# Depthwise conv with 8 rows by 4 column phases of outputs and two column shifts

## The chip, the cores and the metric

The kernel runs on one core of a Trainium2 chip. Its time is the device time of one execution in microseconds (us); the profile is of one execution taken by the hardware profiler. Five engines work in order, each on its own queue: PE (matrix products), DVE, ACT, POOL (elementwise work) and SP (which issues most transfers). Sixteen DMA engines move data between the chip's memory (DRAM) and the on-chip memory.

## The reference, cut to what matters

Input x has 4 images of 128 channels, 128 x 128 pixels. Layer 0 runs attention in overlapping windows of 16 x 16 (step 14, so 9 bands of 9 windows per image), adds x, averages the overlaps (`merged`), and then:

```python
y = _ln(xf, ln2_g, ln2_b)
y = y @ w_p0 + b_p0                       # 128 -> 256 channels
ym = conv_general_dilated(ym, dw_k, window_strides=(1, 1), padding=[(2, 2), (2, 2)],
                          feature_group_count=HIDDEN)      # depthwise, 5 x 5
ym = batchnorm(ym)                        # over images and pixels
y = gelu(gelu(ym)) @ w_p2 + b_p2 + xf     # 256 -> 128 channels
```

Layer 1 has two 3 x 3 convolutions with quantised inputs and weights, each followed by a batch norm; the second adds its input (`identity`).

## The kernel before, in words

Everything is in float32 but layer 1's products, which are in fp8. There are four stages.

*Attention and conv.* A loop runs over 36 bands t, and within it over 9 windows j. The order of work on PE, ACT, DVE and SP is written by hand (`beside`, L881): in each window the scores of j, the values of j-1, and pieces of side work: the first layer norm of the next band (`ln1_chunks`, L478), the output projection, second layer norm and expansion to 256 channels of the band before (`post_chunks`, L531), and tiles of the depthwise conv (`conv_steps`, L615) of an image whose bands are all done. Images 0 and 1 are convolved beside nine bands each, image 2 beside five, and image 3 in three units: rows 0 to 63, 64 to 95 and 96 to 127, the last after the loop (`conv_rest`, L679).

The depthwise conv is done on PE as a banded product. Per channel, the 32 outputs of a column pair are 16 rows by 2 column phases (even, odd); the inputs that they need are 20 rows by 2 phases, `KD` = 40 rows of the contraction. A column shift of -1, 0 and +1 pairs covers the five columns, so there are three products per channel, accumulated in PSUM (`depthwise`, L592), over 8 groups of 16 rows and 64 column pairs, 512 columns. Two channels lie in the two halves of the partitions and four in the four column strips of the array, so eight products run beside each other; a tile (`conv_steps`, at 8 groups) holds 8 channels and 24 matmuls.

The expansion `p0` (L561) takes half a chunk (4 or 3 rows) and half of the channels; ACT adds the bias, splits even and odd columns and writes a tile y (L567; two buffers for each half of the channels, so four), which is stored to y_d in DRAM as rows of 64 values: 256 B pieces. The residual `xf` is stored to xf_d in whole chunks of rows. A conv tile loads its input from y_d (`input_of`, L607; four transfers per tile), ACT copies the result out of PSUM (L648), DVE takes its statistics (L652), and it is stored to cv_d, one 256 B piece for each output row and column phase.

Most transfers are issued by SP, in order. `flush` (L429) issues the stores that a piece of side work left, right after that piece.

*Gelu stage* (`gelu_stage`, L1182 on). 64 units of 8 image rows: load 1 MB of conv result and 0.5 MB of xf, two gelus on ACT, the product back to 128 channels on PE (L1228), bias and residual on DVE (L1236, which also interleaves even and odd columns), quantisation, and layer 1's first conv of the unit two steps earlier (`conv3x3`, L1155; its matmuls are L1164).

*Last stages* (`last_stages`, L1280 on). The second conv once over all units for the statistics, the conv of the unit three steps earlier each time, and then again for images 0 to 2 for the output, adding the identity and storing 0.5 MB per unit.

Of the kernel before, what the change touches and what calls it, by code (L numbers as in the profile page):

```python
# [14 lines left out]
P = 128  # L15
# [16 lines left out]
GR = 16  # L32
CW = P // 2
KD = 2 * (GR + 4)
NCK = 8

# [10 lines left out]
def layers(  # L47
# [42 lines left out]
    y2_d = [dram.tile([P + 4, 2, 2 * P, CW], F32, name=f"y2_d{b}") for b in range(B)]  # L90
    cv_d = [dram.tile([P // GR, 2 * P, GR * P], F32, name=f"cv_d{b}") for b in range(B)]

    dw_d = dram.tile([2 * NCK, KD, 3, 16 * 32], F32, name="dw_d")
    pad_d = dram.tile([2 * GR + 3, 7, 2 * P], F32, name="pad_d")
    band_d = dram.tile([32, 3, KD, 2 * P], F32, name="band_d")
# [74 lines left out]
    units = [(b, 0, P // GR) for b in range(B - 1)] + [(B - 1, g, n) for g, n in ((0, 4), (4, 2), (6, 2))]  # L170
# [14 lines left out]
    with ExitStack() as actx:  # L185
# [18 lines left out]
        y2t = [[y2p.tile([P, RB, 2, CW], F32, name=f"y2_{h}{n}") for n in range(2)] for h in range(2)]  # L204
# [4 lines left out]
        def scratch(n):  # L209

            return up.tile([P, 32 * CW], F32, name="u")[:, :n]

        def band_matrices():
# [6 lines left out]
            def zeros():  # L220
                zero = scratch(2 * 2 * 2 * CW)
                nc.gpsimd.memset(zero, 0.0)
                held["taps"] = taps = scratch(2 * P)[:N_TAPS]
                nc.sync.dma_start(out=taps, in_=dw_k.rearrange("c o i j -> (o i j) c"))
                n = (2 * GR + 3) * 7 * 2 * P // P
                nc.sync.dma_start(
                    out=pad_d.rearrange("y x c -> (y x c)").rearrange("(p n) -> p n", p=P),
                    in_=zero[:, :n],
                )
                held["zero"] = zero  # L230

            def edges(b):
                for d in (y2_d[b][0:2], y2_d[b][P + 2 :]):
                    nc.sync.dma_start(
                        out=d.rearrange("r e c x -> (r e c x)").rearrange("(p n) -> p n", p=P),
                        in_=held["zero"],
                    )

            def padded_taps():
                for dy in range(5):  # L240
                    nc.sync.dma_start(
                        out=pad_d[GR - 1 + dy, 1:6, :], in_=held["taps"][5 * dy : 5 * dy + 5, :]
                    )

            def by_outputs(ro):
                for eo in range(2):

                    nc.sync.dma_start(
                        out=band_d[2 * ro + eo].rearrange("s (r e) c -> s r (e c)", e=2),
                        in_=bass.AP(  # L250
                            pad_d.tensor,
                            pad_d[GR - 1 - ro, 1 - eo, 0:1].offset,
                            [[4 * P, 3], [7 * 2 * P, GR + 4], [1, 4 * P]],
# [32 lines left out]
            pieces = [(c, s) for c in range(0, 2 * P, 64) for s in range(3)]  # L286
            steps = [zeros, *each(edges, [(b,) for b in range(B)]), padded_taps, lambda: None]
            steps += each(by_outputs, [(ro,) for ro in range(GR)])
# [242 lines left out]
        def post_chunks(t, sel=None):  # L531
# [4 lines left out]
            for at, (r, n) in enumerate(finished(t)):  # L536
# [5 lines left out]
                def project(hh, r=r, n=n, at=at, held=held):  # L542
# [9 lines left out]
                    if hh:  # L552
                        store(
                            xf_d[b][:, (i * STEP + r) * P : (i * STEP + r + n) * P],
                            held["xf"][:, : n * P],
                        )
# [4 lines left out]
                def p0(h, hh, r=r, n=n // 2, held=held):  # L561
# [4 lines left out]
                    y2t[h].append(y)  # L566
                    nc.scalar.activation(  # L567
                        y[:, :n],
                        pm[:, : n * P].rearrange("p (r c e) -> p r e c", r=n, e=2),
                        AF.Identity, bias=bp0[:, h : h + 1],  # L570
                    )
                    store(
                        y2_d[b][row + 2 : row + n + 2, :, h * P : (h + 1) * P, :].rearrange(
                            "r e p x -> p (r e) x"
                        ),
                        y[:, :n].rearrange("p r e x -> p (r e) x"),
                    )

# [13 lines left out]
        def depthwise(outs, wt, ut, n):  # L592

            for j in range(n // 4):

                for s, (a, z) in ((1, (0, CW)), (0, (1, CW)), (2, (0, CW - 1))):
                    for half in range(2):
                        hs = slice(64 * half, 64 * half + KD)
                        for q in range(4):
                            c = 4 * j + q  # L600
                            nc.tensor.matmul(  # L601
                                outs[half][32 * q : 32 * q + 32, j, :, a:z],
                                wt[hs, s, c, :], ut[hs, :, c, a + s - 1 : z + s - 1],
                                start=(s == 1), stop=(s == 2),
                            )

        def input_of(b, g, ng, ch, n, a, z):  # L607

            return bass.AP(
                y2_d[b].tensor,  # L610
                y2_d[b][GR * g + a, 0, ch, 0:1].offset,
                [[2 * P * CW, 2 * (z - a)], [GR * 2 * 2 * P * CW, ng], [1, n * CW]],
            )

        def conv_steps(n, ahead=2):  # L615
# [3 lines left out]
            nc_ = min(8, 32 // ng)  # L619
# [4 lines left out]
            def load(at):  # L624
                k, jj, c = tiles[at]
                if c == 0:
                    W[k, jj] = up.tile([P, 3, 8, 32], F32, name="w")
                    weights(W[k, jj], k, jj, 1, nc.sync.dma_start)
                ut = up.tile([P, 32 * CW], F32, name="u")[:, : ng * nc_ * CW]
                U[at] = ut = ut.rearrange("p (g c x) -> p g c x", g=ng, c=nc_)  # L630
                for half in range(2):
                    ch = 32 * k + 16 * half + 8 * jj + c
                    for a, z in ((0, GR), (GR, GR + 4)):
                        nc.sync.dma_start(
                            out=ut[64 * half + 2 * a : 64 * half + 2 * z].rearrange(
                                "p g c x -> p g (c x)"
                            ),
                            in_=input_of(b, g0, ng, ch, nc_, a, z),
                        )

            def products(at):
# [4 lines left out]
                for half in range(2):  # L646
# [4 lines left out]
                    for j in range(nj):  # L651
# [3 lines left out]
                        ch = 32 * k + 16 * half + 8 * jj + c0 + 4 * j  # L655
                        store(
                            bass.AP(
                                cv_d[b].tensor,
                                cv_d[b][g0, ch, 0:1].offset,
                                [[CW, P], [2 * P * GR * P, ng], [1, CW]],  # L660
                            ),
                            cv[:, j],
# [16 lines left out]
        def conv_rest(n, w_t, u_t, c_t):  # L679
# [5 lines left out]
            at = GR + 2  # L685

            def load(k, a, z, g, m):
                for half in range(2):
                    ch = 32 * k + 16 * half
                    nc.sync.dma_start(  # L690
                        out=U[k][64 * half + 2 * a : 64 * half + 2 * z, g : g + m].rearrange(
                            "p g c x -> p g (c x)"
                        ),
                        in_=input_of(b, g0 + g, m, ch, 16, a, z),
                    )

            U = [u_t.tile([P, ng, 16, CW], F32, name=f"u{k}") for k in range(NCK)]
            W = [w_t.tile([P, 3, 16, 32], F32, name=f"w{k}") for k in range(NCK)]
            for k in range(NCK):
                weights(W[k], k, 0, 2, nc.gpsimd.dma_start)  # L700
            for k in range(early):
                load(k, 0, at, 0, 1)

            def late(k):
                if k < early:
                    load(k, 0, at, 1, 1)
                    load(k, at, GR + 4, 0, ng)
                else:
                    load(k, 0, GR, 0, ng)
                    load(k, GR, GR + 4, 0, ng)  # L710

            def step(k):
# [6 lines left out]
                for half in range(2):  # L719
# [9 lines left out]
                    for g in range(ng):  # L729
                        engine.dma_start(  # L730
                            out=bass.AP(
                                cv_d[b].tensor,
                                cv_d[b][g0 + g, 32 * k + 16 * half, 0:1].offset,
# [673 lines left out]
```

## Time and profile before

| | us |
|---|---|
| median of 3 runs | 3246.4 (3238.51 to 3248.32) |
| the profiled execution | 3249.98 |
| its span, first to last instruction | 3248.2 |

| group | count | busy us | mean ns |
|---|---|---|---|
| L1164 PE, layer 1's convs | 3168 | 700.3 | 381 |
| L784 PE, scores | 5184 | 413.6 | 417 |
| L567 ACT, y out of PSUM | 288 | 183.1 | 641 |
| L648 ACT, conv result out of PSUM | 256 | 132.4 | 563 |
| L867 DVE, reciprocal | 324 | 568.8 | 1756 |

A row of a group names the line, the engine, the operation, its output and inputs with their shapes, and how often it ran; then the union of its time, the mean of one, and the idle time of the engine before it with what ended it. PE lists a float32 matmul as two. A row of the timeline has the start, the length, the engine, the operation and, in brackets, how long the engine had been idle and what released it. The DMA share is the mean busy share of the 16 DMA engines. The clock is PE's granted clock, 1.00 being full.

ACT waited for stores of y to land (y_d<-y) 76 times, 111.9 us in all, at most 14.6. Most of the attention stage, from 525 us on, has conv tiles beside it; the gelu stage runs from about 2320 to 2795 us, the second conv's two passes from there to the end.

### The profile page before, as it was taken

How to read it: one execution, taken by the hardware profiler on the slowest of the kernel's cores; microseconds unless marked ns; L12 is line 12 of the kernel's file. 1: busy time of each engine (PE TensorE's matmuls, PEld its weight loads, DVE VectorE, ACT ScalarE, POOL GpSimd, SP SyncE). 2: the span in 40 equal slices, each digit the busy share in tenths (PEclk: the TensorE clock that was granted, in tenths of full speed). 3: DMA queues.
4: the chain of work that ended last, by engine and by line, in shares of the span. 5: the costliest groups of instructions: out<-in, count | busy, mean ns of one | idle time of the engine just before them, and what ended most of it. 6: DMA issues, size and time to landing. Idle time of an engine off the chain costs nothing.

```text
span 3248.2 us, 92154 instructions
## 1 busy us (share of the span) xinstructions
PE 3059.6 (94%) x39162; PEld 1480.1 (46%) x39162; DVE 2014.5 (62%) x3244; ACT 1988.5 (61%) x2658; POOL 840.9 (26%) x1058
## 2 busy tenths in 40 slices
PE   7999999999999999999888998876899999999998
PEld 4555544444444444444344444453544444444443
DVE  5777886766766777676555664542455555666543
ACT  5777777777776777677555655432477777433443
POOL 3444443333333333333222232211111111000000
PEclk9999999999999999999999998876799999999999
DMA  3555677888886888886898988857899999452398
GB/s 82 151 167 162 176 186 191 203 199 204 215 193 169 191 206 211 196 213 172 179 202 201 209 188 203 196 158 187 264 354 359 358 359 304 162 167 80 110 357 311
DMA packets 809891, 681.70 MB, mean 210 GB/s; under 512 B 580918, under 2 KB 695935, under 8 KB 809471
## 3 DMA queue, kind: packets, MB, share of 16 engines
q1 hardware_dynamic: 798879, 669.17, 75.8%
q8 instruction: 311, 5.10, 0.7%
q0 software_dynamic: 1024, 3.93, 0.5%
q10 hardware_dynamic: 9568, 2.61, 0.3%
q14 instruction: 109, 0.89, 0.1%
HBM read 408.72 MB, written 270.79 MB: 209 GB/s over the span
## 4 chain that ended last, share of the span: by engine, by line
PE 76%; DMA 9%; ACT 5%; issue 4%; SPq 3%; DVE 2%; ACTq 0%; POOL 0%; DVEq 0%; POOLq 0%
PE pc L1164 21%; PE pm L438 16%; PE sc L784 9%; PE pm L601 9%; PE po L847 8%; PE pb L1228 6%; PE po L855 3%; DMA y_d<-y 3%; PE pm L377 3%; ACT pt L792 2%; DMA u<-y_d 2%; DMA xn<-row 1%; SPq L451 1%; SPq L431 1%; ACT v L775 1%
## 5 line engine op out<-in xcount | busy, mean ns | idle before, releaser
L867 DVE RECIPROCAL rd<-po 128x256 f32<-128x256 f32 x324 | 568.8, 1756 | 439.1 <-PE po L855 438.5
L1164 PE MATMUL pc<-q,wq 128*128 128x512 fp8e4 x3168 | 700.3, 381 | 5.1 <-DVE q L1176 5.1
L792 ACT ACTIVATE pt<-sc 128x1024 f32<-128x1024 f32 x648 | 628.2, 1025 | 119.1 <-PE sc L784 63.2
L802 POOL TENSOR_TENSOR sm<-pt 128x512 f32<-128x512 f32 x324 | 415.7, 1283 | 1047.3 <-ACT pt L792 727.0
L1164 PEld LDWEIGHTS <-wq 128*128 128x128 fp8e4 x3168 | 309.0, 98 | 406.7 <-issue 38.9
L784 PE MATMUL sc<-q,kr 32*128 32x256 f32 x5184 | 413.6, 417 | 27.3 <-ACT pt L792 27.1
L601 PE MATMUL pm<-u,w 40*32 40x504 f32 (+5 forms) x7680 | 369.6, 503 | 41.7 <-DMA u<-y_d 29.7
L784 PEld LDWEIGHTS sc<-q,kr 32*128 32x128 f32 x5184 | 254.1, 191 | 286.4 <-issue 177.1
L847 PE MATMUL po<-pt,v 128*32 128x256 f32 x5184 | 364.9, 401 | 10.0 <-DVE part L871 6.9
L648 ACT COPY c<-pm 128x512 f32<-128x512 f32 (+1 forms) x256 | 132.4, 563 | 272.3 <-PE pm L601 243.3
L438 PE MATMUL pm<-xn,wp 128*32 128x512 f32 (+1 forms) x2304 | 248.1, 553 | 44.6 <-ACT y L567 42.6
L567 ACT ACTIVATE y<-pm,vectors 128x512 f32<-128x512 f32 (+1 forms) x288 | 183.1, 641 | 166.0 <-DMA y_d<-y 111.9
L802 DVE TENSOR_TENSOR sm<-pt 128x512 f32<-128x512 f32 x324 | 244.2, 754 | 35.8 <-ACT pt L792 35.8
L438 PE MATMUL pm<-xn,wqkv 128*32 128x512 f32 (+1 forms) x2304 | 245.3, 548 | 4.9 <-ACT v L775 3.5
L601 PEld LDWEIGHTS pm<-u,w 40*32 40x32 f32 x7680 | 147.6, 112 | 223.1 <-issue 153.0
L652 DVE BATCH_NORM_STATS2 st<-c 128x6 f32<-128x512 f32 (+2 forms) x320 | 160.9, 550 | 134.8 <-ACT c L648 134.3
L1228 PE MATMUL pb<-cv,wp 128*128 128x512 f32 x512 | 232.1, 596 | 4.9 <-ACT cv L1219 4.9
L847 PEld LDWEIGHTS po<-pt,v 128*32 128x32 f32 x5184 | 140.5, 112 | 186.5 <-issue 103.5
L1172 DVE BATCH_NORM_STATS2 st<-pc 128x6 f32<-128x512 f32 x256 | 165.7, 689 | 84.7 <-PE pc L1164 84.7
L855 PE MATMUL po<-sm,ones 128*32 128x256 f32 x2592 | 206.1, 389 | 0.0
L874 POOL TENSOR_TENSOR ob<-ob,part 128x32 f32<-128x32 f32 x288 | 127.2, 442 | 230.6 <-DVE part L871 224.8
L438 PE MATMUL pm<-wqkv,yr 128*32 128x128 f32 x5184 | 176.3, 273 | 1.2 <-issue 1.2
(157 smaller groups left out, 3394.2 us busy)
## 6 DMA issues: line engine op xcount, KB each, us to landing
cv<-cv_d SPq DMA_DIRECT2D x64, 1024.0 KB
u<-y_d SPq DMA_DIRECT2D x234, 256.0 KB
cv_d<-c SPq DMA_DIRECT2D x192, 256.0 KB
y_d<-y SPq DMA_DIRECT2D x160, 256.0 KB
xn<-row SPq DMA_DIRECT2D x76, 512.0 KB
xfl<-xf_d SPq DMA_DIRECT2D x64, 512.0 KB
id_d<-y SPq DMA_DIRECT2D x64, 512.0 KB
idt<-id_d SPq DMA_DIRECT2D x64, 512.0 KB
```

Source lines behind the costliest of these rows:

```text
L438: nc.tensor.matmul(out[m], w[:, m], v, start=True, stop=True)
L567: nc.scalar.activation(y[:, :n], pm[:, : n * P].rearrange("p (r c e) -> p r e c", r=n, e=2), AF.Identity, bias=bp0[:, h : h + 1],)
L601: nc.tensor.matmul(outs[half][32 * q : 32 * q + 32, j, :, a:z], wt[hs, s, c, :], ut[hs, :, c, a + s - 1 : z + s - 1], start=(s == 1), stop ...
L784: nc.tensor.matmul(sc[h // 2][:, h % 2, kc, :].rearrange("p (r c) -> p r c", c=RS), region(kr, j)[hs, kc * P : (kc + 1) * P], queries(j, h ...
L792: nc.scalar.activation(pt, sc[p], AF.Exp)
L802: add(sm, pt[:, :, 0, :], pt[:, :, 1, :], ALU.add)
L847: nc.tensor.matmul(po[hs, 0, :], v[:, kc, hs], pt[h // 2][:, h % 2, kc, :], start=(kc == 0), stop=(kc == 1),)
L855: nc.tensor.matmul(po[hs, 1, :], ones, sm[h // 2][:, h % 2, :], start=True, stop=True)
L867: nc.vector.reciprocal(rd, po[:, 1, :])
L1164: nc.tensor.matmul(pc[:, h], w[:, t, :], q1[b][:, r + dy : r + dy + RB, dx : dx + P], start=(t == 0), stop=(t == 8),)
L1172: nc.vector.bn_stats(st[:, 2 * n + h, :], pc[:, h])
L1228: nc.tensor.matmul(pb[:, m], wp2[:, h, :], cv[:, h, px], start=(h == 0), stop=(h == 1))
```

## The change

The conv's outputs are 8 rows by 4 column phases (`GR` 16 to 8, `NC` 4), its inputs 12 rows by 4 phases (`KD` 40 to 48), and two column shifts cover the five columns: two products for three. A channel of an image has 16 groups of 8 rows and 32 column quads, again 512 columns.

y_d has the order phase and row in the group, channel, group, 33 columns; a tile y has four phases of 33 columns in each row, with one zero column for the border, and each piece that is stored is 33 values, 132 B. Two of the four phases are written by ACT, two by DVE. A store that crosses a group of 8 rows is cut in two. A tile of the conv's input is, for whole images, one contiguous run of 4 channels x 17 groups x 33 columns on each partition (`fetch_input`). The conv's result goes to cv_d with 8 groups of one output row and phase side by side (1 KB pieces for whole images and rows 0 to 95 in part, 512 B for the last rows). xf_d has its rows in the same order, so it is stored in rows of 512 B.

In the later stages a unit of 8 rows is then the rows with the same place in their group (rows 0, 8, 16 ... of half an image). q1's rows are laid out so that the conv's neighbours are again contiguous blocks (`first_row`), the units run in the order 7, 0, 1, ... 6 in each half, the conv follows four units later (`LAG`) instead of two or three, and the output is stored in rows of 512 B.

```diff
-GR = 16
-CW = P // 2
-KD = 2 * (GR + 4)
+GR = 8
+NG = P // GR
+NC = 4
+CW = P // NC
+CX = CW + 1
+KD = NC * (GR + 4)
 NCK = 8
+LAG = 4
...
-    y2_d = [dram.tile([P + 4, 2, 2 * P, CW], F32, name=f"y2_d{b}") for b in range(B)]
-    cv_d = [dram.tile([P // GR, 2 * P, GR * P], F32, name=f"cv_d{b}") for b in range(B)]
+    y2_d = [dram.tile([NC * GR, 2 * P, NG + 1, CX], F32, name=f"y2_d{b}") for b in range(B)]
+    cv_d = [dram.tile([2, 2 * P, 32, NG // 2, CW], F32, name=f"cv_d{b}") for b in range(B)]
...
+                        row = i * STEP + r
+                        cut = min(n, GR - row % GR)
+                        for a, z in ((0, cut), (cut, n)):
+                            if z > a:
+                                g, ro = divmod(row + a, GR)
+                                store(
+                                    xf_d[b].rearrange("p (h o g c) -> p h o g c", h=2, o=GR, c=P)[
+                                        :, g // 8, ro : ro + z - a, g % 8, :
+                                    ],
+                                    held["xf"][:, a * P : z * P].rearrange("p (r c) -> p r c", c=P),
+                                )
...
+                    to = y[:, :n].rearrange("p r (a f x) -> p r a f x", a=2, x=CX)
+                    by = pm[:, : n * P].rearrange("p (r x a f) -> p r a f x", r=n, a=2, f=2)
                     nc.scalar.activation(
-                        y[:, :n],
-                        pm[:, : n * P].rearrange("p (r c e) -> p r e c", r=n, e=2),
-                        AF.Identity, bias=bp0[:, h : h + 1],
+                        to[:, :, 0, :, :CW], by[:, :, 0], AF.Identity, bias=bp0[:, h : h + 1]
                     )
-                    store(
-                        y2_d[b][row + 2 : row + n + 2, :, h * P : (h + 1) * P, :].rearrange(
-                            "r e p x -> p (r e) x"
-                        ),
-                        y[:, :n].rearrange("p r e x -> p (r e) x"),
+                    nc.vector.tensor_scalar(
+                        to[:, :, 1, :, 1:], by[:, :, 1], bp0[:, h : h + 1], None, ALU.add
                     )
+                    cut = min(n, GR - (row + 2) % GR)
+                    for a, z in ((0, cut), (cut, n)):
+                        if z > a:
+                            g, r0 = divmod(row + 2 + a, GR)
+                            store(
+                                y2_d[b][NC * r0 : NC * (r0 + z - a), h * P : (h + 1) * P, g, :].rearrange(
+                                    "q p x -> p q x"
+                                ),
+                                y[:, a:z].rearrange("p r (q x) -> p (r q) x", x=CX),
+                            )
...
-                for s, (a, z) in ((1, (0, CW)), (0, (1, CW)), (2, (0, CW - 1))):
+                for s in range(2):
                     for half in range(2):
                         hs = slice(64 * half, 64 * half + KD)
                         for q in range(4):
                             c = 4 * j + q
                             nc.tensor.matmul(
-                                outs[half][32 * q : 32 * q + 32, j, :, a:z],
-                                wt[hs, s, c, :], ut[hs, :, c, a + s - 1 : z + s - 1],
-                                start=(s == 1), stop=(s == 2),
+                                outs[half][32 * q : 32 * q + 32, j],
+                                wt[hs, s, c, :], ut[hs, c, : outs[half].shape[2], s : s + CW],
+                                start=(s == 0), stop=(s == 1),
                             )
...
+        def fetch_input(ut, b, g, ch, below):
+            n, ng = ut.shape[1:3]
+            rows = 4 if below else GR
+            for half in range(2):
+                to = ut[64 * half + NC * GR * below : 64 * half + NC * (GR * below + rows)]
+                src = y2_d[b][0 : NC * rows, ch + 16 * half : ch + 16 * half + n]
+                if ng > NG:
+                    m = (n * ng - below) * CX
+                    nc.sync.dma_start(
+                        out=to.rearrange("p c g x -> p (c g x)")[:, :m],
+                        in_=bass.AP(src.tensor, src.offset + below * CX, [src.ap[0], [1, m]]),
+                    )
...
-                                [[CW, P], [2 * P * GR * P, ng], [1, CW]],
+                                [[8 * CW, P], [2 * P * 32 * 8 * CW, gh], [1, ng // gh * CW]],
...
+    def first_row(k):
+        return {-1: 0, GR - 1: 1, 0: NG + 1, GR: NG + 2}.get(k, NG + 2 + NG * k)
...
-                if n >= 2:
-                    pc = conv3x3(ps_c, n - 2, wq[0])
+                if n >= LAG:
+                    pc = conv3x3(ps_c, n - LAG, wq[0])
...
-                if n >= 3:
-                    b, k = units[n - 3]
-                    pc = conv3x3(ps_d, n - 3, wq[1])
+                if n >= LAG:
+                    b, k = conv_units[n - LAG]
+                    pc = conv3x3(ps_d, n - LAG, wq[1])
...
-                    out=out[b, :, 2 * RB * k : 2 * RB * (k + 1), :].rearrange("c r w -> c (r w)"), in_=z
+                    out=out[b, :, k // GR * 64 + k % GR : k // GR * 64 + 64 : GR, :],
+                    in_=z.rearrange("p (r w) -> p r w", w=P),
```

Beside these, the preparation in the first ten bands follows the layout: 64 copies that build the bands of taps for 32, eight pieces of weights for twelve, zeros written to the borders of y_d in 132 B pieces, and the four y tiles cleared once at the start.

## The prediction

> **What bounds the kernel now.** I read the page first (shares, transfers, groups), then the busy time by stretches, then the timeline at the end of one band and at one long stall, and last the transfer records grouped by size.
>
> ```profile
> span 3248.2 us, 92154 instructions
> ...
> PE 3059.6 (94%) x39162; PEld 1480.1 (46%) x39162; DVE 2014.5 (62%) x3244; ACT 1988.5 (61%) x2658; POOL 840.9 (26%) x1058
> ...
> DMA packets 809891, 681.70 MB, mean 210 GB/s; under 512 B 580918, under 2 KB 695935, under 8 KB 809471
> ...
> L601 PE MATMUL pm<-u,w 40*32 40x504 f32 (+5 forms) x7680 | 369.6, 503 | 41.7 <-DMA u<-y_d 29.7
> ```
>
> PE is the bound, and the depthwise conv (L601) holds 369.6 us of it, with 75.6 us more in a group of its own at the end of attention. But most transfers are under 512 B: 539,648 of 256 B, half the stores of y, half those of the conv's result.
>
> ```profile
> 525.00:1015.00 490.00, 481.26 (x7786) 227.66 (x7776) 347.88 (x542) 353.21 (x536) 180.17 (x228) 1.00 0.84 198
> ...
> 1640.00:1930.00 290.00, 267.17 (x4120) 122.95 (x4118) 172.91 (x266) 175.44 (x269) 83.34 (x107) 0.95 0.89 204
> ...
> 2200.00:2330.00 130.00, 86.12 (x1961) 58.20 (x1958) 43.87 (x181) 37.75 (x54) 17.97 (x38) 0.63 0.75 200
> ...
> 3045.00:3248.00 203.00, 193.38 (x892) 86.46 (x889) 82.30 (x81) 78.91 (x67) 0.55 (x1) 0.99 0.86 311
> ```
>
> The columns are length, then PE, PEld, DVE, ACT, POOL busy, the clock, the DMA share and GB/s. While image 0 is convolved (from 525) PE is idle 9 us in 490, at a DMA share of 0.84 (0.87 in its full bands). Where image 2 goes through in five bands (from 1640), the share is 0.89 and PE loses 23 us and 5% of its clock. So the conv stretch lies close to a second limit, the transfers.
>
> ```profile
> 903.77 1.76 DVE L867 RECIPROCAL rd<-po 128x256 f32<-128x256 f32 x1 [0.66 <-PE po L855]
> ...
> 903.93 3.62 PE L438 MATMUL pm<-xn,wp 128*32 128x512 f32 x32
> ...
> 906.57 1.08 DVE L421 TENSOR_TENSOR xn<-xn,xf 128x384 f32<-128x384 f32 x2
> ...
> 908.73 9.95 SPq L431 DMA_DIRECT2D y_d<-y  x8
> ...
> 916.84 0.58 ACT L567 ACTIVATE y<-pm,vectors 128x384 f32<-128x384 f32 x1 [1.46 <-DMA y_d<-y]
> ...
> 917.71 0.58 ACT L567 ACTIVATE y<-pm,vectors 128x384 f32<-128x384 f32 x1 [0.29 <-DMA y_d<-y]
> ...
> 919.75 1.94 ACT L792 ACTIVATE pt<-sc 128x1024 f32<-128x1024 f32 x2 [0.61 <-ACT rstd L392]
> ...
> 920.83 0.70 PE L784 MATMUL sc<-q,kr 32*128 32x256 f32 x4 [0.60 <-ACT pt L792]
> ```
>
> This is the end of a band: eight products (L438 xn,wp), eight tiles y, eight stores that SP needs 10 us to issue. With four y buffers, the fifth to eighth y wait for the first four stores, ACT runs late into its exponentials, and PE waits for those. In a denser band the same wait is long:
>
> ```profile
> 1696.94 0.98 PE L438 MATMUL pm<-xn,wp 128*32 128x384 f32 x8 [4.48 <-ACT y L567]
> 1697.84 2.09 PE L784 MATMUL sc<-q,kr 32*128 32x256 f32 x16
> ```
>
> After 4.48 us of idleness the scores take 2.09 us for the usual 1.15: a stall also costs clock.
>
> The transfer records give, as medians, 9 ns for 4 B, 18 for 256 B, 27 for 512 B, 46 (lowest tenth) for 1024 B, 159 for 4096 B, 309 (lowest tenth) for 8192 B. These lie on 9 + 0.0366 x bytes.
>
> **The change part by part.** The sum is made against the profiled run, 3249.98 us (span 3248.2), 3.6 above the median of 3246.4; I set it against the median.
>
> A, the conv's third shift removed. A full tile's 24 matmuls take 2.78 us; 16 take two thirds, 0.9 less. Images 0 to 2 have 96 tiles, 86 us; image 3 has as many columns as each of them, 29 more: -115. Bounds: -77 (0.2 us of each tile is start and stays; 96 x 0.6 plus a third) to -148 (a third of 369.6 + 75.6).
>
> B, savings that meet another wait. In the band above one of some 3.7 tiles (917.38) stands right before scores that wait 0.60 us for ACT, so its 0.9 is lost: 115/3.7 is 31, and where the wait is absent nothing: +25 (0 to +40).
>
> C, the band's end. Half of each y goes from ACT to a new DVE instruction; the nearest row, 256 columns out of PSUM (L384), takes 414 ns. It is queued behind rd, ob, part, sm, xn, which end at 907.65. The fourth product needs the psum bank of the first (three banks, one gone to v), so it starts at 908.06 where PE stood ready at 906.5: 1.5 us of stall. The eighth likewise waits for the DVE y behind sm (914.22), 0.6 us. Both are partly the same time as the wait for stores. Those grow: each y is now 2048 packets of 132 B for 1024 of 256 B. Four stores take 4 x 2048 x 13.8/16 ns = 7.1 us by the line above, 9.7 us at 19 ns (the mean of 256 B), against 4.9. Issued from 908.73, the fourth lands near 917.3 or 919.9 with some 1.5 us of latency; the eighth y comes at 917.71 now. So the exponentials at 919.75 come 0 to 2.4 us later; I take 1.0, for 26 bands with conv beside them: +26 (0 to +62).
>
> D, all transfers of an ordinary conv band (57.4 us at share 0.87, 50 us of 16 engines). y: 14336 packets, 12.4 us by the line, 17.0 at 19 ns, for 8.5. Conv results: 1869 packets of 1 KB at 46 to 50 ns for 7475 of 256 B: -3.1. Input tiles: 350 runs of 8976 B at 337 ns (1.3 times that under load, as 4096 B has mean 196 for 159) for 2336 of 1 KB at 79: -1.9. Weights -0.5. The residual in 512 B rows: +1.1. Together -0.5 or +4.1 us. At the first, nothing: 0, bounds -20 and +60. Image 2's five bands have 6.6 tiles each, so the relief there is larger, -4.9 or -0.3 a band, and PE's 23 us of idleness there shrink: -15 (-40 to 0). SP issues 368 y stores for 288 and 112 residual stores for 72, 120 x 0.4 us over 36 bands; the row load at 920.88 is queued behind the y stores and xn waits for it, inside the +60.
>
> 132 B lies between the rows of 4 B and 256 B, so I take the line through both, 13.8 ns. The Trainium skill (DMA: Bandwidth & Descriptors, section How a descriptor splits into AXI transactions) speaks against it: a read that doesn't start on a multiple of 256 B fetches from the boundary below. Pieces at a pitch of 132 B would then cost about what 256 B cost, and the sum would be that of the slower rival below. No run here shows unaligned reads of this size; the 128 writes of 1960 B, off any such boundary, have a median of 81 ns, on the line.
>
> E, the first ten bands: DVE's extra y in groups of two or three, no conv to save: 10 x 0.7 = +7 (0 to +15). The 64 band copies for 32, the edge stores in 132 B pieces and four memsets lie beside a share of 0.58; without that cover they are some 10 us.
>
> F, the tail (2200 to 2330): eight y stores dearer by 8 x 0.65 = +5, input runs of 528 B for 4 KB +1 each for the first, conv_rest's eight steps shorter and half the result stores: 0 (-12 to +12).
>
> G, gelu stage: the conv starts two units later; two units run at ACT's pace (2 x 1.235 + 1.911 = 4.4 us) in place of PE's 3.4: +3 with the end (0 to +6). The strided addition has 746 ns now at stride 2 and stays covered by PE's 7.34 us a unit even at double.
>
> H, last stage: outputs in 512 B rows, 65,536 x 27/16 ns = 111 us for 93 us, in 200 us at share 0.86; plus 1.4 us for a unit more of lag: +8 (0 to +20).
>
> Sum: -115 + 25 + 26 + 0 - 15 + 7 + 0 + 3 + 8 = -61; 3246 - 61 = **3185 us**.
>
> **The rivals.** *Transfers become the bound, slower.* For: share 0.89 already costs PE 23 us in 290. Against: the line. At 19 ns an ordinary band needs 54.1 us of the engines. No stretch of one band holds a share over 0.92 now, so it lasts 58.8 us, +1.4, x 18 = +25; image 2's bands -1.7 x 5 = -8; E 10, H 20, G 3, F 12: +62, **3308 us**. It decides from about 17.5 ns a packet on, where work over 0.92 is the old 57.4. More than 19 ns takes it further up.
>
> *The gain in full.* C and B are absorbed by slack of ACT and DVE (61 and 62% busy): -115 - 15 + 7 + 3 + 8 = -112, **3134 us**. Against: PE waits for ACT at each band's end today.
>
> *It goes into waits, no change*, **3246 us**: the band's end at its dear bound (+62) with B at +40.
>
> **How the numbers follow.** Gain in part 0.40 (own range 3140 to 3228), in full 0.15, no change 0.07, transfers bound 0.38. Faster by over 0.3% (10 us, about what these runs can tell) 0.55, within 0.07, slower 0.38. The range 3130 to 3325 holds the first, no change, three quarters of the slower case and half of the full one: 0.83.
>
> **What would show it.** L601 at two thirds of its busy time; median of 132 B packets near 14 (not 18 or more); DMA share in the first conv bands at or under 0.90; waits of DVE's and ACT's y for y_d not above twice the 111.9 us of ACT now. PE's granted clock under 0.97 between 525 and 1500, or DMA shares of 0.95 there, would make me wrong.

## The result, and the profile after

The changed kernel takes **4407.2 us** (median of 4 runs, 4402.2 to 4419.4) against 3244.1 for the kernel before on the same chip (3238.5 to 3248.3): a ratio of **1.359** [1.356, 1.363]. The forecast was 3185, and the range ended at 3325. The sign and the size are wrong.

The page of the kernel after, its parts 1, 2, 4 and 5:

```profile
span 4400.4 us, 86617 instructions
...
PE 3291.9 (75%) x36090; PEld 1496.4 (34%) x36090; DVE 2175.4 (49%) x3524; ACT 1948.3 (44%) x2658; POOL 838.7 (19%) x1062
...
PEclk9867788788788877887788777778776799999999
DMA  3996799999999999999999999999989999965279
...
DMA packets 1006631, 702.95 MB, mean 160 GB/s; under 512 B 624718, under 2 KB 911511, under 8 KB 997015
...
DMA 38%; PE 37%; DVE 8%; ACT 7%; issue 5%; SPq 4%; POOL 1%; ACTq 0%; DVEq 0%; POOLq 0%
DMA y_d<-y 22%; PE pc L1201 10%; PE pm L451 7%; DMA xn<-row 6%; PE sc L811 5%; PE pm L629 5%; PE po L874 4%; DMA row<-rstd 4%; PE pb L1265 3%; SPq L444 2%; DMA u<-y_d 2%; PE po L882 2%; ACT cv L1253 2%; DVE rd L894 2%; DMA xr<-in_x_dram 2%
...
L629 PE MATMUL pm<-u,w 48*32 48x512 f32 (+2 forms) x5120 | 391.6, 625 | 364.0 <-DVE y L593 116.7
...
L590 ACT ACTIVATE y<-pm,vectors 128x256 f32<-128x256 f32 (+1 forms) x288 | 131.1, 455 | 970.5 <-DMA y_d<-y 841.1
L593 DVE TENSOR_SCALAR y<-pm,vectors 128x256 f32<-128x256 f32 (+1 forms) x288 | 124.0, 449 | 826.5 <-ACT y L590 826.4
```

Every compute engine is less busy as a share, while the DMA row is at nine tenths or more in nearly every slice from the sixth to the end of attention, with 160 GB/s over the span where it was 210. So the engines of the transfers are full and move less. The chain of waits names the transfer: stores of y are 22% of the span. ACT waited 841 us for them (112 before) and DVE, which writes the other half of each y, waited for ACT for nearly the same time (826 us). The conv (L629, a third fewer matmuls) has a little more busy time than L601 had, because each one is longer: 625 ns for 503.

The end of a band on the timeline of the kernel after (start, length, engine, work, in brackets the idle time before and its releaser):

```profile
1002.66 1.25 DVE L593 TENSOR_SCALAR y<-pm,vectors 128x256 f32<-128x256 f32 x3
1003.16 34.12 SPq L444 DMA_DIRECT2D y_d<-y  x8
...
1016.43 0.42 ACT L590 ACTIVATE y<-pm,vectors 128x192 f32<-128x192 f32 x1 [7.28 <-DMA y_d<-y]
...
1022.30 0.42 ACT L590 ACTIVATE y<-pm,vectors 128x192 f32<-128x192 f32 x1 [5.44 <-DMA y_d<-y]
...
1028.23 0.42 ACT L590 ACTIVATE y<-pm,vectors 128x192 f32<-128x192 f32 x1 [5.50 <-DMA y_d<-y]
...
1029.16 3.64 PE L629 MATMUL pm<-u,w 48*32 48x512 f32 x24 [4.60 <-DVE y L593]
...
1034.33 0.42 ACT L590 ACTIVATE y<-pm,vectors 128x192 f32<-128x192 f32 x1 [5.68 <-DMA y_d<-y]
```

The fifth to eighth y each wait for one of the first four stores, and these land 5.9 us apart. A store of four rows is 2048 pieces of 132 B, so 2048/5.9, about 345 pieces a microsecond, is what this write gets from all 16 engines. The first y of this group comes 13 us after the first issue, the last 31; in the band shown before, the last came 9 us after. The ordinary conv bands (10 to 27, counted from 0, from the starts of their first reciprocals) take 88.5 us each, where they took 57.35.

The same stretches as in the prediction, and one of the late stages (length, PE, PEld, DVE, ACT, POOL busy, clock, DMA share, GB/s):

```profile
525.00:1015.00 490.00, 339.26 (x4516) 159.94 (x4512) 256.23 (x405) 221.20 (x339) 126.27 (x157) 0.81 1.07 119
1640.00:1930.00 290.00, 205.89 (x2664) 90.51 (x2668) 137.08 (x221) 128.00 (x200) 65.70 (x84) 0.80 1.12 130
3400.00:4400.00 1000.00, 949.77 (x4462) 422.49 (x4452) 587.10 (x867) 512.29 (x419) 74.51 (x83) 0.97 0.78 260
```

PE is idle for 31% of the conv stretch and its clock is 0.81. A DMA share above 1.00 means that records of packets on one engine overlap. The late stages, where every piece has 512 B or more, take nearly as long as before: from the first product of the gelu stage to the end 950 us, where it was 929. A transfer record has the size, start and length of one packet. The records by size tell which transfers are dear:

```
                        pieces    10th/50th/90th percentile   mean ns   16 engines, us
before   256 B         539,648    16 / 18 /  19                19.0        641
after    132 B         558,592    14 / 14 / 136                57.8       2017
after    512 B         148,096    27 / 27 /  27                28.6        265
```

Sixteen engines' time is the sum of the records divided by 16. The median of the 132 B pieces is the 14 ns of the prediction's line. Their mean is four times that, and the mean is what is paid.

### The profile page after: what moved, and what is told of

It is laid out like the page before. It is cut to its first block, busy times and chain, and to the rows that moved or that the text cites. A ratio compares the mean times of both kernels' runs of the same rounds, so it can differ in the third digit from the quotient of the medians.

```text
span 4400.4 us, 86617 instructions
## 1 busy us (share of the span) xinstructions
PE 3291.9 (75%) x36090; PEld 1496.4 (34%) x36090; DVE 2175.4 (49%) x3524; ACT 1948.3 (44%) x2658; POOL 838.7 (19%) x1062
## 3 DMA queue, kind: packets, MB, share of 16 engines
q0 software_dynamic: 1024, 3.15, 0.4%
## 4 chain that ended last, share of the span: by engine, by line
DMA 38%; PE 37%; DVE 8%; ACT 7%; issue 5%; SPq 4%; POOL 1%; ACTq 0%; DVEq 0%; POOLq 0%
DMA y_d<-y 22%; PE pc L1201 10%; PE pm L451 7%; DMA xn<-row 6%; PE sc L811 5%; PE pm L629 5%; PE po L874 4%; DMA row<-rstd 4%; PE pb L1265 3%; SPq L444 2%; DMA u<-y_d 2%; PE po L882 2%; ACT cv L1253 2%; DVE rd L894 2%; DMA xr<-in_x_dram 2%
## 5 line engine op out<-in xcount | busy, mean ns | idle before, releaser
L819 ACT ACTIVATE pt<-sc 128x1024 f32<-128x1024 f32 x648 | 628.2, 1024 | 203.8 <-PE sc L811 79.6
L629 PE MATMUL pm<-u,w 48*32 48x512 f32 (+2 forms) x5120 | 391.6, 625 | 364.0 <-DVE y L593 116.7
L811 PE MATMUL sc<-q,kr 32*128 32x256 f32 x5184 | 491.7, 470 | 200.9 <-ACT pt L819 200.8
L590 ACT ACTIVATE y<-pm,vectors 128x256 f32<-128x256 f32 (+1 forms) x288 | 131.1, 455 | 970.5 <-DMA y_d<-y 841.1
L593 DVE TENSOR_SCALAR y<-pm,vectors 128x256 f32<-128x256 f32 (+1 forms) x288 | 124.0, 449 | 826.5 <-ACT y L590 826.4
L811 PEld LDWEIGHTS sc<-q,kr 32*128 32x128 f32 x5184 | 296.6, 217 | 528.5 <-ACT pt L819 291.8
L874 PE MATMUL po<-pt,v 128*32 128x256 f32 x5184 | 419.7, 449 | 48.8 <-DVE part L898 46.9
L451 PE MATMUL pm<-xn,wp 128*32 128x512 f32 (+1 forms) x2304 | 275.0, 588 | 228.6 <-DVE y L593 217.6
L629 PEld LDWEIGHTS pm<-u,w 48*32 48x32 f32 x5120 | 109.3, 123 | 571.3 <-issue 226.0
L882 PE MATMUL po<-sm,ones 128*32 128x256 f32 x2592 | 228.2, 424 | 0.8 <-issue 0.8
L434 DVE TENSOR_TENSOR xn<-xn,xt 128x384 f32<-128x384 f32 (+1 forms) x140 | 81.8, 626 | 278.1 <-DMA xn<-row 278.1
```

What stands on the lines that cost most here:

```text
L451: nc.tensor.matmul(out[m], w[:, m], v, start=True, stop=True)
L629: nc.tensor.matmul(outs[half][32 * q : 32 * q + 32, j], wt[hs, s, c, :], ut[hs, c, : outs[half].shape[2], s : s + CW], start=(s == 0), sto ...
L811: nc.tensor.matmul(sc[h // 2][:, h % 2, kc, :].rearrange("p (r c) -> p r c", c=RS), region(kr, j)[hs, kc * P : (kc + 1) * P], queries(j, h ...
L819: nc.scalar.activation(pt, sc[p], AF.Exp)
L874: nc.tensor.matmul(po[hs, 0, :], v[:, kc, hs], pt[h // 2][:, h % 2, kc, :], start=(kc == 0), stop=(kc == 1),)
L882: nc.tensor.matmul(po[hs, 1, :], ones, sm[h // 2][:, h % 2, :], start=True, stop=True)
```

## The experiments

All kernels were compared with the kernel before on their own chip; the ratios are against that. cx32 and the shifts by 4, 32 and 64 B ran twice, the others four times or more.

| kernel | us | ratio, interval |
|---|---|---|
| cx32: after, pieces of 128 B | 3341.2 | 1.029 [1.020, 1.038] |
| shift4: before, y_d moved by 4 B | 3740.2 | 1.152 [1.144, 1.159] |
| shift16: by 16 B | 3598.5 | 1.111 [1.109, 1.114] |
| shift32: by 32 B | 3286.7 | 1.012 [1.007, 1.017] |
| shift64: by 64 B | 3291.1 | 1.014 [1.009, 1.019] |
| before_halves: 128 B pieces, twice the stores | 3373.2 | 1.039 [1.035, 1.042] |
| before_rows: 256 B pieces, twice the stores | 3276.5 | 1.012 [1.010, 1.015] |
| before_2shift: no third shift | 3207.8 | 0.991 [0.988, 0.994] |
| halves_2shift: both | 3317.8 | 1.024 [1.021, 1.027] |
| cx32_act: y by ACT alone | 3329.5 | 1.024 [1.021, 1.027] |
| cx32_pool: band copies on POOL's queue | 3312.7 | 1.020 [1.017, 1.023] |
| before_out: results in rows of 512 B | 3244.5 | 0.999 [0.998, 1.001] |
| before_q: half the y stores on ACT's queue | 3272.8 | 1.007 [1.004, 1.010] |
| 2shift_q: that, and no third shift | 3244.6 | 0.999 [0.998, 1.001] |
| cx32_pq: cx32_pool, half the y stores on ACT's queue | 3359.0 | 1.033 [1.032, 1.035] |

**What makes the pieces slow.** Three theories: they start and end inside an aligned unit of DRAM; each lies 2.2 KB from the next; there are too many of them. cx32 is the changed kernel with 32 columns for 33. Pieces become 128 B on 128 B boundaries, with their number and their scatter kept; the zero column and the second shift are left out of what is computed.

```diff
-CX = CW + 1
+CX = CW
-    to[:, :, 1, :, 1:], by[:, :, 1], ...
+    to[:, :, 1, :, :CW], by[:, :, 1], ...
-    ut[hs, c, : outs[half].shape[2], s : s + CW],
+    ut[hs, c, : outs[half].shape[2], :CW],
```

> The changed kernel with 32 columns for 33 in y, so every stored piece is 128 B at a multiple of 128 B, with the same number of pieces and the same scatter (the border column and the shift by one column are left out, so the border and the second product's data are not the reference's). Theory 1 (pieces that start or end inside an aligned unit of DRAM are slow to write, and the queue backs up behind them): the mean of a piece falls from 57.8 ns to 13 to 20, the time to 3150 to 3350 us. Theory 2 (each piece lands in another DRAM row, pitch about 2.2 KB, where before 128 channels lay side by side): mean stays over 45 ns, time 4200 to 4450. Theory 3 (twice as many small pieces is what costs, wherever they land): the same as theory 2.

The shifts are the opposite edit: the kernel before with its y_d begun 1, 4, 8 or 16 values later, its 256 B pieces otherwise the same. The loads of y_d are displaced with it.

```diff
-    y2_d = [dram.tile([P + 4, 2, 2 * P, CW], F32, ...) ...]
+    y2_r = [dram.tile([(P + 4) * 2 * 2 * P * CW + 64], F32, ...) ...]
+    y2_d = [r[1 : 1 + (P + 4) * 2 * 2 * P * CW].rearrange(...) for r in y2_r]
```

> The kernel before with all of y_d moved by 4 B in DRAM: 256 B pieces, as many as before and side by side as before, but each starts and ends inside an aligned unit. Theory 1: the pieces of y become slow (at the some 350 per us that the changed kernel's stores settle at, a band's 7168 take 20 us for 8), ACT's waits for y_d grow from 112 us to several hundred, time 3400 to 3800 us. Theories 2 and 3: no change, 3230 to 3265.

> The kernel before with y_d moved by 32 B. Theory 1 with a unit of 64 B or more: slow like the shift by 4 B. Theory 1 with a unit of 32 B: unchanged, 3230 to 3265. Theories 2 and 3: unchanged.

> The kernel before with y_d moved by 64 B. Theory 1 with a unit of 64 B: unchanged, 3230 to 3265; with a unit of 128 or 256 B: slow like the shift by 4 B. Theories 2 and 3: unchanged.

> The kernel before with the conv's input moved by 16 B in DRAM: its 256 B pieces start on 16 B boundaries that are not 32 B boundaries. Moved by 4 B it took 3740 us (mean piece 39.6 ns), by 32 B 3287 (22.0 ns). If the unit of a write is 32 B: 3700 to 3780 and 36 to 42 ns. If it is 16 B or less: 3275 to 3300 and 21 to 24 ns.

cx32 gives back 1066 of the 1163 us. Its waits for the stores and for DVE's y (us, times, longest), and then its conv group:

```profile
ACT y L590 <- DMA y_d<-y: 143.1, 82, 12.4
...
PE pm L451 <- DVE y L593: 82.5, 58, 7.9
```

```profile
L629 PE MATMUL pm<-u,w 48*32 48x512 f32 (+2 forms) x5120 | 270.8, 525 | 64.9 <-DMA u<-y_d 39.0 <-DMA cv_d<-c 11.7 <-DVE xf L562 9.1
```

ACT's wait falls from 841 us to 143, the conv group to 270.8 (two thirds of 369.6 would be 246), and the 128 B pieces have a mean of 14.4 ns. And 4 B of displacement alone brings the whole symptom into the kernel before. The same wait (us, times, longest) in shift4:

```profile
ACT y L570 <- DMA y_d<-y: 447.7, 128, 19.6
```

and in shift16 and shift32, in this order:

```profile
ACT y L570 <- DMA y_d<-y: 351.1, 119, 20.8
```

```profile
ACT y L570 <- DMA y_d<-y: 139.2, 78, 17.5
```

The mean of the 256 B pieces is 39.6 ns moved by 4 B, 34.8 by 16, 22.0 by 32, 21.7 by 64, and 19.0 in place. So the unit of a write is **32 B**: of the displacements tried, those by a multiple of 32 B are cheap, the others are not. Scatter and number are out as the main cause, since cx32 kept both. The displaced loads are out too: the packets of 1024 B, most of which are these loads, have a mean of 80.6 ns in shift4 for 77.6 before. Off a 256 B boundary, but on 32 B, the pieces cost a further 1.2 to 1.4%, where I had expected no change. I had expected shift16 at 3700 or more if the unit is 32 B; it came to 3598, so a cut at 16 B is cheaper than one at 4 B, for a reason that these runs don't show.

The cost goes by the piece rather than by its bytes. Of shift4's 539,648 pieces of 256 B, 262,144 are y's (4 images x 128 rows x 2 phases x 256 channels). If the others kept 19.0 ns, each of y's has a record (39.6 - 19.0) x 539,648/262,144 = 42 ns longer; that of a 132 B piece is 57.8 - 14.4 = 43 ns longer than that of one of 128 B. In time, 497 us over 262,144 and 1066 us over 558,592 are both 1.9 ns a piece. In shift4's ordinary bands the displaced pieces settle at 292 to 300 a microsecond, near the 345 of the kernel after, though they are twice as long; in cx32 up to 1500 go. Nor is it needed that neighbours are written at the same time: in shift4 the pieces that share a unit are channels of one store, in the kernel after rows 8 apart, from different stores, and the extra cost of a record is the same.

The Trainium skill says at two places what would bear on this. *Collectives: The Full Stack*, in its Rules for kernel authors, wants the buffers of collectives aligned to 32 bytes, since otherwise the hardware reads, modifies and writes back; the runs at 4, 16 and 32 B agree with that boundary, for ordinary stores too, though no run shows the reading: the bytes read from DRAM are counted as 408.72 MB in the kernel before and in shift4 alike. *DMA: Bandwidth & Descriptors*, in its Specifications, puts the read-modify-write at anything below 512 B. Here 128 B and 256 B pieces in whole units took 14.4 and 19.0 ns, close to the line through the smallest and largest sizes (13.7 and 18.4), and no such step shows.

**What is left at 128 B.** cx32 is still 2.9% slower than the kernel before, with a third of the conv's work gone. before_halves and before_rows cut each y store of the kernel before in two, by columns and by rows.

```diff
-    store(y2_d[b][rows, :, channels, :]..., y[:, :n]...)
+    for x in (slice(0, 32), slice(32, 64)):
+        store(y2_d[b][rows, :, channels, x]..., y[:, :n, :, x]...)
```

> The kernel before, with each y store cut into two, of columns 0 to 31 and 32 to 63: twice as many pieces, 128 B each, all on 128 B boundaries, and nothing else. Theory (aligned pieces cost only their own engine time, 14.4 ns against 19, which other work covers): 3240 to 3260. Rival (twice the pieces are part of the loss by themselves): 3270 to 3330, with the wait of ScalarE's y for its own store above 130 us.

> The kernel before, with each y store cut into two by rows: twice as many stores for SyncE's queue, but the same 256 B pieces in the same number. The cut by columns, which doubled stores and pieces both, gave 3373 us against 3249. Theory (it is the number of pieces): 3243 to 3275. Rival (it is the number of stores that SyncE's queue has to issue): 3330 to 3390, with bands 2 to 5 at 54 to 60 us each, as there, against 46 to 49 in the kernel before.

Twice the stores cost 1.2%, and halving the pieces 2.6% more. I had expected nothing from aligned 128 B pieces as such: the rival holds, with ACT's wait at 169 us, and 3373 us is beyond even its 3330. before_rows came out between its two sides: the time (3276.5) is at the upper end of the theory's range, but bands 2 to 5 grew as the rival said, 219 us for 193; there SP also issues the copies for the band matrices. Its ordinary bands stay at 57.2. With halved pieces the ordinary bands go to 60.1 as well.

cx32_pool and cx32_act take out two suspected costs of the change (both leave out the same as cx32).

```diff
-    nc.sync.dma_start(out=band_d[NC * ro + eo]...)
+    nc.gpsimd.dma_start(out=band_d[NC * ro + eo]...)
```

> The kernel with 128 B pieces (border column and second shift left out of the computation), with the 64 copies that build the band matrices issued from GpSimd's queue in place of SyncE's. Bands 0 to 9 took 567 us there and 502.5 in the kernel before. Theory (the copies hold up SyncE's queue, behind which the y stores and loads stand): bands 0 to 9 fall by 25 to 50 us, the time from 3341 to 3290 to 3316. Rival (the transfers themselves, or the edge stores, or the waits for y, cost it): bands 0 to 9 fall by less than 12 us and the time stays at 3325 to 3355.

```diff
-    nc.scalar.activation(to[:, :, 0, ...], by[:, :, 0], ...)
-    nc.vector.tensor_scalar(to[:, :, 1, ...], by[:, :, 1], ...)
+    nc.scalar.activation(to, by, ...)
```

> The kernel with 128 B pieces, with the whole of y by ScalarE in one instruction for each product (VectorE's share of y taken out); as there, the border column and the second shift are left out of the computation. It was 3341 us (span 3329.6), with 58.1 us for each ordinary conv band and 80.8 us of TensorE's waits for VectorE's y. Theory (what is left over the kernel before is VectorE's y standing in TensorE's way): the wait for VectorE's y is gone, ordinary bands fall to 55 to 57 us, and the time to 3280 to 3315. Rival (it is the number of pieces, or the accesses of the copies, and the wait moves to ScalarE's y): ordinary bands stay at 57.5 to 59 and the time at 3325 to 3360.

The copies cost some 0.9%, though the two intervals overlap: band 10 starts at 544 us for 567, against 502.5 before. The 23 us are just under the theory's 25 to 50. DVE's half of y costs little: without it the time is 0.5% less, within the intervals. In cx32_act the wait that PE had for DVE's y became a wait for ACT's:

```profile
ACT y L590 <- DMA y_d<-y: 169.5, 90, 15.9
...
PE pm L451 <- ACT y L590: 53.3, 19, 14.8
```

The rival held: a wait moved, and the ordinary bands stayed (58.25 us for 58.00).

**What the third shift is worth.** before_2shift leaves out the third product of the conv and nothing else; halves_2shift does it with the halved stores.

```diff
-    for s, (a, z) in ((1, (0, CW)), (0, (1, CW)), (2, (0, CW - 1))):
+    for s, (a, z) in ((1, (0, CW)), (0, (1, CW))):
```

> The kernel before, with the third of the conv's three column shifts left out of the computation (a third of the conv's matmuls), its loads, stores and pieces as they were. Predicted for this part of the change: -115 us (-77 to -148), that is 3096 to 3170, likeliest 3130. Rival (transfers and other engines stand right behind TensorE, so most of it is not to be had): 3200 to 3245, ordinary bands above 56.5 us where the saving in full would make them 54 or less.

> Two edits of the kernel before at once: each y store cut into two of columns 0 to 31 and 32 to 63 (3373 us by itself), and the conv's third shift left out of the computation. Theory (with 128 B pieces the bands follow the transfers and the stores, so TensorE's saving is worth little there): 3335 to 3373. Rival (the two add): 3373 less what leaving out the third shift alone gives, that is 3225 to 3300 if that is 77 to 148.

The saving alone is **31 us**, not 115. With halved pieces it is 1.039 less 1.024, so 1.5% or some 48 us, less than 77 and more than the theory's nothing to 38: neither side was right. One stretch of the kernel before, then the same of before_2shift:

```profile
520.00:1500.00 980.00, 961.64 (x15444) 455.71 (x15440) 685.01 (x1062) 703.93 (x1064) 357.64 (x453) 0.99 0.85 199
```

```profile
520.00:1500.00 980.00, 937.87 (x14670) 446.92 (x14664) 693.41 (x1085) 714.94 (x1080) 364.87 (x461) 0.98 0.84 202
```

PE's idle time in the stretch goes from 18 to 42 us: 24 us of the saving turned into waiting there, and DVE, ACT and POOL did only 1 to 2% more work in the same time. The ordinary bands went from 57.35 to 56.46 us, 16 us over 18 bands, where two images' share of the term was 58; image 2's five bands gave 9 for 29. Image 3, a good part of whose conv has no attention beside it, kept more: the last bands and all that follows are 20 us shorter, for 29. (These come from one profiled run each, of different chips, and add up to some 14 us more than the medians do.)

**Is it the queue of the stores?** In before_2shift ACT still waits 118 us for y's stores and PE 49 for ACT's y. I took SP's queue for the next limit and gave half of the y stores to ACT's queue, in the kernel before, in before_2shift and in cx32_pool.

```diff
-    store(y2_d[...], y[...])
+    store(y2_d[...], y[...], nc.scalar if h else None)
```

> The kernel before, with the y stores of the second half of the channels issued from ScalarE's queue in place of SyncE's. Theory (TensorE is the bound here, the stores' queue only close behind it): 3215 to 3250. Rival (issuing costs ScalarE's own work more than the queue gains): 3250 to 3300.

> As the last, and the conv's third shift left out of the computation, which alone gave 3208 us (31 us less than the kernel before). Theory (y's stores in SyncE's queue hold back what TensorE saves): 70 us or more under the last one, that is 3130 to 3175, ordinary bands at 55 us or less. Rival (something else stands behind TensorE: the two engines' other waits, the transfers): 20 to 45 us under the last one, ordinary bands at 56 or more.

> The form with 128 B pieces and the band copies on GpSimd's queue (3313 us; border column and second shift left out of the computation), with the y stores of the second half of the channels issued from ScalarE's queue. Theory (the twice as many pieces cost through the queue that issues and lands them one after another): 3230 to 3285. Rival (through the 16 engines' time or the waits for VectorE's y): 3300 to 3330.

This theory fell. All three are slower than with SP alone, by 0.7, 0.8 and 1.3%, and the third shift is worth 0.75% there, against 0.9% alone. For the first two the rivals hold; cx32_pq, at 3359 us, lies above both of its ranges. In 2shift_q ACT's waits for the stores are fewer and longer:

```profile
ACT y L567 <- DMA y_d<-y: 126.9, 31, 14.4
...
PE pm L438 <- ACT y L567: 93.9, 23, 13.4
```

They are no shorter in sum (127 us for 118), and PE's wait for y rose from 49 to 94 us. In the other two ACT's waits did fall (103 us for 112, 87 for 118), and PE's wait for y rose all the same (71 us for 43, 92 for 75). The edit has a price of its own: the 144 stores that ACT issues hold its queue for 59 us in before_q. So it shows that this way of sharing does not pay, not that SP's queue is free of blame. What exactly stands behind PE in an ordinary band is open.

**The results' rows.** before_out stores the output in rows of 512 B at a pitch of 4 KB; each row of the result is put at another place.

```diff
-    out=out[b, :, 2 * RB * k : 2 * RB * (k + 1), :].rearrange("c r w -> c (r w)"), in_=z
+    out=out[b, :, k // 8 * 64 + k % 8 : k // 8 * 64 + 64 : 8, :], in_=z.rearrange("p (r w) -> p r w", w=P)
```

> The kernel before, with its results stored in rows of 512 B that lie 4 KB apart in the output (each result row is put elsewhere, so the output is in another order), in place of 4 KB runs. Predicted for the change: +8 us (0 to 20), that is 3244 to 3263. Rival: the late stages of the run with 128 B pieces ended 20 us later than before for this reason: 3258 to 3270. Third: covered entirely, 3240 to 3246.

No difference: 0.999 [0.998, 1.001], as the third side said.

No run beats the kernel before but before_2shift, which computes less. A form of the change that computes everything with whole units could, for instance, pad each piece to 40 columns for 33; no run has one.

## Why the prediction was wrong, point by point

**D failed, at one sentence:** "132 B lies between the rows of 4 B and 256 B, so I take the line through both, 13.8 ns." The line holds for 128 B in whole units (14.4 ns) and not for 132 B (57.8). Of the 1222 us between forecast and result, 1066 are this price. Size was the only axis on which I interpolated. The lower end of the line was no such store at all: the 288 more stores of before_rows brought 4608 more packets of 4 B, 16 for each, so these rows come with every transfer and most of them are not data of the kernel. My second support, 128 writes of 1960 B off any 256 B boundary at a median of 81 ns, did cut units (1960 is not a multiple of 32); its fault is that a median over a few pieces says nothing of a queue that fills. The records show it filling: in the band above some 2600 pieces start from 1005 to 1010 us, at up to 820 a microsecond, with a mean of about 25 ns; from then on they settle near 345 a microsecond, with a mean of 70 ns.

The rival "transfers become the bound, slower" was the right mechanism, and "more than 19 ns takes it further up" the right direction; its price was bounded by 19 ns, the mean of an aligned 256 B piece, as if a small piece could not cost more than a larger one. That bound set the range's upper end. The cited rule on reads off a 256 B boundary pointed the right way and gave the same low price.

**The signs to look for:** the predicted median near 14 came true and proved nothing. The busy time of L629 was 391.6 us, far from two thirds of 369.6. The others answered plainly: DMA shares above 0.95, the clock at 0.81, ACT's wait 7.5 times as long. I had named a median where only the mean, or the 90th percentile, could speak.

**A was mis-sized:** 31 us for 115. The count of instructions was right (5120 for 7680), and so was the time of PE that they hold: all of the conv was busy for 413.4 us before and for 299.5 in before_2shift, 114 less. (The 75.6 us of the last group are a misreading, two overlapping rows added up; it is busy for 43.8, so A's far bound should have been -138.) What failed is that PE, busy for 98% of the stretch, was taken for its bound: beside attention less than a third of the saving due there came out, at the tail two thirds. B, +25, was this doubt and should have been some +84; as I tied it to one wait in one band, it was bounded at 40. (The rival without a change, by its own terms, adds up to 3236 and not 3246.)

**C and D's other half, the number of pieces:** D added up engine time (12.4 us a band for 8.5) and let a share under 0.92 hide it. Halving aligned pieces lengthened an ordinary band by 2.75 us, of which twice the stores gave none. C allowed 1.0 us a band for it, at most 2.4. The part of C that is DVE's is small (cx32_act).

**E was mis-sized:** +7, where cx32 loses 64 us up to band 10. I had put the band copies "beside a share of 0.58", as if a low share were cover. SP's queue is a good part of it: moving the copies off it gave back 23 us there, and doubled stores cost 26 us there even in the kernel before. The rest of the 64 no run divides.

**G and H:** the strided addition on DVE went from 746 to 1160 ns in cx32 and POOL's wait for it from 392 to 400 us. Whether it is covered as said isn't shown: a unit of the gelu stage takes 7.55 us there for 7.34, and the stage 471 us for 463, more than G's bound of 6. H's +8 is nothing by itself (before_out), yet the last stages take 478 us in cx32 for 467. No run here divides these 20 us.

Added up, each by its own ratio, the parts come near: +3.9% (halved pieces and doubled stores; cx32 has 368 y stores for 288) - 1.5% (the shift, with halved pieces) + 0.9% (the copies) = +3.3%, against cx32's 2.9%. They come from other kernels, so this is a check and no proof. The remaining 1066 us are the 32 B unit.

## What to carry to other kernels

Before a layout with a pad or an odd pitch is stored to DRAM, work out the first and last byte of each piece: unless both are multiples of 32 B, each of some hundred thousand pieces may cost 1.4 to 1.9 ns of the kernel's time, as here, which came to some nine times the 115 us that the pad was to save. Judge packets by their mean and 90th percentile, never by the median, and price an unseen access from a row that shares its alignment, not only its size. An engine that is busy 98% of the time in a stretch may still give back only some quarter of what is taken off it, as here; one run that leaves the work out tells how much.

## What the runs showed of the hardware

- Writes to DRAM that cut a 32 B unit 4 B (or a multiple of it) off have records some 42 ns longer than whole ones in the mean, at 132 B as at 256 B. Once a first burst has passed (2600 pieces in the band shown), all engines together write some 345 a microsecond of 132 B, 45 GB/s, and 292 to 300 of 256 B displaced by 4 B.
- Starting off a 256 B boundary, but on 32 B, raises the mean of all 256 B pieces, of which about half were moved, from 19.0 to 21.7 and 22.0 ns, and the kernel's time by 1.2 to 1.4%.
- A cut at 16 B costs less than one at 4 B: 34.8 ns for 39.6 in the mean.
- Sharing the y stores between the queues of SP and ACT made the kernel 0.7 to 1.3% slower; an issue took ACT 0.41 us of its queue in before_q.
- A transfer brings packets of 4 B of its own: 16 for each store added in before_rows.
